# A two-layer graph network in one kernel: order of work at the ends of layer 0's chunks, PSUM of the stage between the layers, and the place of the last split

## The chip, the cores and the metric

The kernel runs on one NeuronCore of a Trainium2 chip. The core has a matrix engine (TensorE, PE in the profile, with its weight loads shown apart as PEld), a vector engine (VectorE, DVE), an activation engine (ScalarE, ACT), a general engine (GpSimd, POOL) and the sync engine (SyncE, SP), which here issues nearly all DMAs. Work passes through SBUF (128 partitions) and through PSUM[...], into which TensorE writes. The metric is the device time of one execution in microseconds; lower is better.

## What is computed

Layer 0 is attention over all 4096 rows with a dense additive bias, layer 1 a graph attention with eight heads of 64. Cut to what matters:

```python
# layer 0
h = relu(layernorm(x))                      # x: 4096 x 512, adj: 4096 x 4096
q, k, v = h @ Wq.T + bq, h @ Wk.T + bk, h @ Wv.T + bv
x = x + softmax(q @ k.T / sqrt(512) + adj + adj, axis=-1) @ v
# layer 1, heads n of 64
h = relu(layernorm(x))
nX = heads(h @ W)
nX = a_ln * (nX - mean(nX)) / (std(nX, ddof=1) + 1e-6) + b_ln
at1, at2 = nX @ a1, nX @ a2                 # one number per row and head
kg = leaky_relu(at1[:, None] + at2[None, :], 0.2) * adj
y = softmax(where(adj != 0, kg, -32768), axis=-1) @ nX + nX
x = x + elu(y)
```

## The kernel before

**Tiling.** Rows are handled in 8 chunks (`NI`) of 512 (`GC`), columns in 32 blocks (`NB`) of 128 (`P`). `seq` keeps the instructions it wraps in program order on their engine, so the order of the calls below is the order on each engine and on each DMA queue. Tiles come from pools; a tag with `bufs=n` has n buffers that rotate. A pool opened in the room of a closed one waits for the closed one's last users.

**Projections** (up to line 546): the values, the products of queries and keys, and their sums for a Strassen-like scheme are made and written to DRAM. Their pool's last stores are the `q_d` stores of line 477.

**Layer 0** (lines 547 to 789) goes over all chunks, and in each over 16 pairs of column blocks. For a pair `s`, `stage(s, n, w)`, n = 0 to 3, forms the logits: seven products of half size go to the two halves of one PSUM bank, `xz` (`w["z"]` and `w["x"]`), and `add_part` (line 593, DVE) adds them to the transposed adjacency tile `aT`; `exponent0` (line 597, ACT) makes probabilities; `pair_sums` (lines 609 to 621, POOL) makes sums of them and the running row totals. `weighted(s, ...)` (line 636, PE) adds the pair's products into seven PSUM accumulators `M1` to `M7`, which stay for a whole chunk. The loop interleaves: while pair s is weighted, pair s + 2 passes its four stages, and the tiles of s + 4 and s + 5 are transposed (`swap`, line 324) and prepared for layer 1 (`for_layer_1`, lines 575 to 579, DVE, with two stores each). Where the first pair is concerned, its stages run alone, before the loop.

**Chunk end.** At a chunk's last pair, `chunk_end` puts six parts into the list `ends`, each one or two operations that combine M1 to M7 into rows of the result (line 691: the first on ACT, the others on DVE). `end()` runs the next one. In the last pair they run after stage 0, after stage 1, before the weighted products of M6 and M3, and after stage 3; the last two in the next pair. `total_of_rows` (lines 709 to 719) sums the row totals over partitions with four tiny products against `ones`, into a tile of M6's tag, and takes reciprocals; it runs in the next chunk's first pair, after the sixth part, and for the last chunk after the loop. `divide` (lines 679 to 688) scales the rows and adds x by a DMA.

**Stage between the layers** (lines 1221 to 1258): for each block r of 128 rows: `turn` (transposes, then a relu on ACT), `project` (16 matmuls into `ys[r]`, two banks, tag "l" with two buffers), `variance` (square on ACT, then lines 1110 and 1111 on DVE, then a power of -1/2 on POOL, line 1112), `standardize` (lines 1119 to 1134 on DVE, then line 1139 on POOL, the tile `own`). The order in the loop is turn(r + 1), project(r), standardize(r - 1), variance(r). Tasks hang at blocks (`at_block`): `split(ic)` (lines 1147 to 1169, fourteen DVE steps on a chunk's at1 and at2), `sides(ic, b)` (line 1181 on PE, line 1186 on ACT, three stores each, lines 1188 and 1192), `fours` (lines 1196 to 1200), `load_targets` (line 1204, four loads of `at2m`), stores of features and own rows (lines 1210 and 160). Those of the last chunk that come after block 32 are moved with `at_step` to the first steps of layer 1.

**Layer 1** (from line 1267) has 512 steps: chunk, group of four heads, block. Step n: `sums` (PE, lines 874 and 904, into PSUM tiles l, r0, r1), the tasks of `left`, `left_sums(n + 1)` (line 884), `right_leaky` (line 922, DVE), `right_weigh` (line 928, POOL), `left_relu` (line 890, ACT), `values` of step n - 4 (line 947, PE), tasks marked "mid", `left_weigh` (line 931, DVE), `exponent` (line 935, ACT), tasks marked "end". Every four steps SP issues the loads of the next four (`load_adj`, lines 815 to 830: z2, nb, nx, g; two buffers each), and in the first 32 steps also the features `nX` (line 1058).

## Time and profile before

Median of 3 runs: 3674.54 us (3672.04 to 3674.67). The profiled execution took 3674.76 us; its span, which all times below are counted in, is 3672.7 us.

| what | value |
|---|---|
| PE busy | 3551.3 us, 97% of the span |
| DVE busy | 2548.8 us, 69% |
| POOL busy | 2263.0 us, 62% |
| ACT busy | 1745.0 us, 48% |
| mean rate of all DMAs | 217 GB/s |
| costliest on PE | L947, `values`, 1009.9 us |
| costliest on POOL | L928, `right_weigh`, 1223.1 us |
| stage between the layers | about 1861 to 2036 us |

A line such as "L691 DVE TENSOR_TENSOR x<-x,M" names the kernel's line, the engine, the operation and the tiles it writes and reads. "[0.57 <-DVE x L691]" behind an instruction says how long its engine stood idle before it and which instruction let it go. Such a name is inferred from the times of the events. Busy shares are means over stretches that have different limits, so the reading below goes stretch by stretch. Matmul ends are modelled: an idle time between two runs of matmuls is counted from the modelled end of the first, while a steady row of them starts at shorter distances than its durations.

### The profile page before, as it was taken

Reading aid. Unit: us, or ns where it says so; the run is one execution under the profiler, and the core shown is the slowest. Engines: PE = TensorE matmul, PEld = TensorE weight load, DVE = VectorE, ACT = ScalarE, POOL = GpSimd, SP = SyncE. Lnnn points to the kernel's source line nnn. Section 1 sums busy time; section 2 is a strip of 40 time slices with the busy share of each in tenths; the row PEclk is TensorE's granted clock in tenths of the full one; section 3 lists DMA queues with packets and bytes.
Section 4 is the critical chain, followed back from the end, with each engine's and each line's share of the span. In section 5 each row is a group of like instructions: output and inputs, shape, how many; then the busy total and the mean of one; then the engine's idle time right before and its main releaser. Section 6 shows DMA issues by size and latency. Waiting matters only on the chain. (4 is left out here: it accounts for less than half of the span.)

```text
span 3672.7 us, 58831 instructions
## 1 busy us (share of the span) xinstructions
PE 3551.3 (97%) x21482; PEld 2084.0 (57%) x21482; DVE 2548.8 (69%) x4195; ACT 1745.0 (48%) x1541; POOL 2263.0 (62%) x1770
## 2 busy tenths in 40 slices
PE   8998999999999999999988799999999999999998
PEld 3447888888888888888866223322222223322332
DVE  5435565666666665656556678888888888888887
ACT  1000111111111111111123589998999999989997
POOL 4653445454545454444445568887888888877886
PEclk9999999999999999999999899999999999999999
DMA  6567788888888888888758987887787787778775
GB/s 213 180 207 203 230 242 239 238 242 244 237 234 250 237 237 243 241 249 232 217 143 207 214 220 211 211 212 201 211 209 212 203 213 204 209 198 214 211 210 151
DMA packets 667530, 796.85 MB, mean 217 GB/s; under 512 B 86816, under 2 KB 489696, under 8 KB 658016
## 3 DMA queue, kind: packets, MB, share of 16 engines
q1 hardware_dynamic: 655136, 759.64, 73.6%
q0 software_dynamic: 10704, 31.98, 4.8%
q8 instruction: 171, 2.80, 0.3%
q10 hardware_dynamic: 1392, 1.38, 0.1%
q14 instruction: 127, 1.04, 0.1%
HBM read 602.28 MB, written 182.71 MB: 214 GB/s over the span
## 5 line engine op out<-in xcount | busy, mean ns | idle before, releaser
L928 POOL TENSOR_TENSOR t<-t,g 128x1024 f32<-128x1024 f32 x512 | 1223.1, 2398 | 318.0 <-DVE t L922 242.4
L947 PE MATMUL acc<-t,nX 128*64 128x512 f32 x4096 | 1009.9, 609 | 0.0
L935 ACT ACTIVATE t<-t 128x2048 f32<-128x2048 f32 (+1 forms) x527 | 976.6, 1854 | 0.2 <-POOL t L928 0.2
L922 DVE SCALAR_TENSOR_TENSOR t<-u,at2m,r 128x512 f32<-128x512 f32 x1024 | 718.6, 743 | 209.3 <-issue 145.3
L597 ACT ACTIVATE aT<-aT 128x512 f32<-128x512 f32 x256 | 161.2, 630 | 1415.7 <-DVE aT L593 1415.7
L593 DVE TENSOR_TENSOR aT<-aT,XZ 128x256 f32<-128x256 f32 x896 | 352.9, 417 | 596.8 <-PE XZ L585 592.4
L931 DVE TENSOR_TENSOR t<-l,g 128x1024 f32<-128x1024 f32 x512 | 622.5, 1216 | 20.7 <-DMA g<-gT_d 16.7
L890 ACT ACTIVATE l<-l 128x1024 f32<-128x1024 f32 x512 | 516.5, 1009 | 149.4 <-PE l L884 101.5
L947 PEld LDWEIGHTS acc<-t,nX 128*64 128x64 f32 x4096 | 248.0, 136 | 458.3 <-issue 450.7
L585 PE MATMUL XZ<-qt,hS 128*128 128x256 f32 x2048 | 488.2, 382 | 9.6 <-DVE aT L593 9.6
L585 PEld LDWEIGHTS XZ<-qt,hS 128*128 128x128 f32 x2048 | 390.6, 191 | 64.1 <-DVE aT L593 11.1
L609 POOL TENSOR_TENSOR S<-aT 128x256 f32<-128x256 f32 x128 | 93.0, 726 | 525.8 <-ACT aT L597 525.8
L585 PE MATMUL XZ<-qt,hT 128*128 128x256 f32 x1536 | 374.3, 380 | 4.6 <-DVE aT L593 3.8
L621 POOL TENSOR_TENSOR total<-total,aT 128x256 f32<-128x256 f32 x360 | 326.5, 919 | 9.4
L585 PEld LDWEIGHTS XZ<-qt,hT 128*128 128x128 f32 x1536 | 291.3, 190 | 47.9 <-DVE aT L593 7.2
L874 PEld LDWEIGHTS <-z 6*128 6x128 bf16 x2048 | 52.4, 91 | 433.1 <-DVE t L922 350.2
L610 POOL TENSOR_TENSOR aT<-aT 128x256 f32<-128x256 f32 x128 | 93.0, 726 | 287.3 <-ACT aT L597 287.3
L636 PE MATMUL M<-v,aT 128*128 128x256 f32 x1024 | 263.0, 379 | 0.0
L636 PE MATMUL M<-tv,aT 128*128 128x256 f32 x1024 | 262.7, 379 | 0.0
L636 PE MATMUL M<-v,S 128*128 128x256 f32 x1024 | 242.0, 379 | 0.0
L577 DVE SCALAR_TENSOR_TENSOR gs<-ng,aT 128x512 f32<-128x512 bf16 x256 | 225.7, 882 | 8.8
L884 PE MATMUL l<-z_left,z 64*64 64x512 bf16 x2048 | 203.0, 383 | 26.8 <-DVE t L931 17.1
(178 smaller groups left out, 4372.0 us busy)
## 6 DMA issues: line engine op xcount, KB each, us to landing
g<-gT_d SPq DMA_DIRECT2D x128, 1024.0 KB
ag<-in_adj_dram SPq DMA_DIRECT2D x256, 256.0 KB
hS<-s_d SPq DMA_DIRECT2D x64, 1024.0 KB
gT_d<-gs SPq DMA_DIRECT2D x256, 256.0 KB
nb<-nT_d SPq DMA_DIRECT2D x128, 512.0 KB
nx<-nT_d SPq DMA_DIRECT2D x256, 256.0 KB
hT<-h_d SPq DMA_DIRECT2D x64, 768.0 KB
tv<-vt_d SPq DMA_DIRECT2D x128, 384.0 KB
```

What stands on the lines that cost most here:

```text
L577: seq(nc.vector.scalar_tensor_tensor(gs, ng, G_MASKED / NEG_BIG, aT, ALU.mult, ALU.add))
L585: seq(nc.tensor.matmul(out, a, b, start=start and k == 0, stop=k == 1, skip_group_check=not start,))
L593: seq(nc.vector.tensor_add(p, p, part))
L621: seq(nc.gpsimd.tensor_add(t, t, a))
L636: seq(nc.tensor.matmul(sums[ic][i][:, u, :], a[:, ts(u, P)], b, start=jt == 0 and u == 0, stop=jt == NB - 2, skip_group_check=u == 1,))
L884: seq(nc.tensor.matmul(lefts[n][ts(c, HD), r, :], loads[n // JB][2][ts(r, HD), jt % JB * P + c * HD :][:, :HD], groups[ic, hg]["z1_left"][ ...
L890: seq(nc.scalar.activation(lefts[n], lefts[n], AF.Relu, scale=4.0))
L922: seq(nc.vector.scalar_tensor_tensor(t[:, 2 + e, :], u4[:, e, :], at2m[:, jt, h : h + 1], right[e], ALU.max, ALU.add))
L928: seq(nc.gpsimd.tensor_mul(t[:, 2:4, :], t[:, 2:4, :], both_heads(n)))
L931: seq(nc.vector.tensor_mul(logits[n][:, 0:2, :], lefts.pop(n), both_heads(n)))
L935: seq(nc.scalar.activation(t, t, AF.Exp))
L947: seq(nc.tensor.matmul(grp["acc"][hf][ts(e, HD), :], nX[jt // SB][:, jt % SB, hg * HG + 2 * hf + e, :], t[:, hf + 2 * e, :], start=jt == 0 ...
```

## The change

- `ones` is made once at the start, outside the pool of layer 0.
- The first pair of all gets its `z` in a bank of its own (M3's tag), so its products alternate between two banks.
- In a chunk's last pair the third part of the chunk end runs after stage 3, directly before the fourth. `total_of_rows` runs after stage 2 instead of before it, and M3's weighted products come ahead of M6's. For the last chunk `total_of_rows` uses the `xz` bank and runs before the remaining parts.
- The stage between the layers gets a PSUM pool of its own: one bank for the transposes, three pairs of banks for the projections, one bank for `sides` and `fours`. It is closed before layer 1's pool is opened.
- In `variance` the division by 63 moves into the square's scale; the lower bound 1e-30 is taken on POOL, ahead of the power, and no longer on DVE.
- The last chunk's `split` runs at the end of step 1 of layer 1; its store of at2 at step 2, `fours` and the first `sides` at step 3, the other three `sides` in the middle of steps 5, 7 and 9 in the bank of r1, `load_targets` at step 5.

```diff
@@ -126,6 +126,8 @@
     HB = HD + 1
     back = const.tile([P, 2, HB], F32, name="back")
 
+    ones = const.tile([P, 1], F32, name="ones")
+    nc.vector.memset(ones, 1.0)
     low0 = const.tile([P, SB], F32, name="low0")
     high0 = const.tile([P, SB], F32, name="high0")
     nc.vector.memset(low0, -LOWEST)
@@ -547,8 +549,6 @@
         with tc.tile_pool(name="attn", bufs=2) as work, tc.tile_pool(
             name="attn_ps", bufs=2, space=PSUM
         ) as psum:
-            ones = work.tile([P, 1], F32, name="ones", tag="ones", bufs=1)
-            nc.vector.memset(ones, 1.0)
             later = {}
             turned, probs, sums, rows_of, totals = {}, {}, {}, {}, {}
 
@@ -646,13 +646,14 @@
 
 
                 if n == 0:
-                    w["z"], w["x"] = xz[:, 0], xz[:, 1]
+                    w["x"] = xz[:, 1]
+                    w["z"] = w["alone"] if "alone" in w else xz[:, 0]
                     product(w["z"], s, "A12", "B21", True)
                     product(w["x"], s, "A11", "B11", True)
                     add_part(s, 0, w["z"])
                     add_part(s, 0, w["x"])
                 elif n == 1:
-                    product(w["z"], s, "S1", "T1", False)
+                    product(w["z"], s, "S1", "T1", "alone" in w)
                     product(w["x"], s, "S2", "T2", False)
                     add_part(s + 1, 1, w["z"])
                     add_part(s, 1, w["x"])
@@ -707,7 +708,10 @@
                     rests.append(divide)
 
             def total_of_rows(ic):
-                pt4 = psum.tile([P, 2, H], F32, name="pt4", tag="M6", bufs=1)[:, 0, 0:SB]
+                if ic + 1 < NI:
+                    pt4 = psum.tile([P, 2, H], F32, name="pt4", tag="M6", bufs=1)[:, 0, 0:SB]
+                else:
+                    pt4 = xz[:, 0, 0:SB]
                 total = totals.pop(ic)
                 for b in range(SB):
                     seq(nc.tensor.matmul(
@@ -723,7 +727,7 @@
                 swap(s)
                 for_layer_1(s)
             load_sums(0)
-            w = {}
+            w = {"alone": psum.tile([P, 2, H], F32, name="z0", tag="M3", bufs=1)[:, 0]}
             for n in range(4):
                 stage(0, n, w)
             pair_sums(0)
@@ -763,15 +767,13 @@
                     stage(s + 2, 1, w)
                 end()
                 weighted(s, (4, 1), (5, 0), (5, 1))
-                if jt == 0 and ic:
-                    total_of_rows(ic - 1)
                 if more:
                     stage(s + 2, 2, w)
                 if jt == NB - 4 and ic + 1 < NI:
                     load_chunk(ic + 1, nc.sync, range(4, 7))
-                if last_pair:
-                    end()
-                weighted(s, (6, 0), (6, 1), (3, 0), (3, 1))
+                if jt == 0 and ic:
+                    total_of_rows(ic - 1)
+                weighted(s, (3, 0), (3, 1), (6, 0), (6, 1))
                 if ahead:
                     swap(s + 5)
                     for_layer_1(s + 5)
@@ -779,13 +781,14 @@
                     stage(s + 2, 3, w)
                 if last_pair:
                     end()
+                    end()
                 if more:
                     pair_sums(s + 2)
                 for f in later.pop(s, []):
                     f()
+            total_of_rows(NI - 1)
             while ends:
                 end()
-            total_of_rows(NI - 1)
             rests[0]()
 
 
@@ -796,7 +799,8 @@
         name="ga_in", bufs=2
     ) as inputs, tc.tile_pool(name="gat", bufs=1) as gat, tc.tile_pool(
         name="ga", bufs=2
-    ) as work, tc.tile_pool(name="ga_ps", bufs=2, space=PSUM) as psum:
+    ) as work, ExitStack() as banks:
+        psum = banks.enter_context(tc.tile_pool(name="stage_ps", bufs=2, space=PSUM))
         JB = 4
         STEPS = [(ic, hg, jt) for ic in range(NI) for hg in range(NH // HG) for jt in range(NB)]
         n_steps = len(STEPS)
@@ -1084,14 +1088,13 @@
             seq(nc.sync.dma_start(out=xns[ic], in_=by_blocks(xn_d, ic)))
 
         def turn(r):
-            tag = f"r{r % 2}"
-            m = psum.tile([P, GC], F32, name=tag, tag=tag, bufs=1)
+            m = psum.tile([P, GC], F32, name="turned", tag="turned", bufs=1)
             for k in range(KC):
                 seq(nc.tensor.transpose(m[:, ts(k, P)], xns[r // SB][:, r % SB, ts(k, P)], ident))
             seq(nc.scalar.activation(h1s[:, r % 2], m, AF.Relu))
 
         def project(r):
-            ys[r] = psum.tile([P, 2, GC], F32, name="l", tag="l", bufs=2)
+            ys[r] = psum.tile([P, 2, GC], F32, name="y", tag="y", bufs=3)
             for g in range(2):
                 for k in range(KC):
                     seq(nc.tensor.matmul(
@@ -1102,14 +1105,15 @@
         def variance(r):
             ic, b = r // SB, r % SB
             seq(nc.scalar.activation(
-                sqs[:, r % 2].rearrange("p (g h) e -> p g (h e)", g=2), ys[r][:, :, 0 : D // 2], AF.Square
+                sqs[:, r % 2].rearrange("p (g h) e -> p g (h e)", g=2), ys[r][:, :, 0 : D // 2],
+                AF.Square, scale=1.0 / math.sqrt(HD - 1.0),
             ))
             v = prep.tile([P, NH], F32, name="var", tag="var", bufs=2)
             root = prep.tile([P, NH], F32, name="pw", tag="pw", bufs=2)
             deviating[r] = v, root
             seq(nc.vector.tensor_reduce(v, sqs[:, r % 2], AX.X, ALU.add))
-            seq(nc.vector.tensor_scalar(v, v, 1.0 / (HD - 1.0), 1e-30, ALU.mult, ALU.max))
-            seq(nc.gpsimd.tensor_tensor(root, v, mhalf[:, 0:NH], ALU.pow))
+            seq(nc.gpsimd.tensor_scalar_max(root, v, 1e-30))
+            seq(nc.gpsimd.tensor_tensor(root, root, mhalf[:, 0:NH], ALU.pow))
 
         def standardize(r):
             ic, b = r // SB, r % SB
@@ -1150,9 +1154,13 @@
             at2s = prep.tile([P, SB, NH], F32, name="at2s", tag="at2s", bufs=2)
             seq(nc.vector.tensor_scalar_mul(at2s, at[:, :, 1, :], -4.0))
             rows = slice(ic * SB, (ic + 1) * SB)
-            at_block(SB * ic + 5, lambda: seq(nc.sync.dma_start(
-                out=at2_d[rows].rearrange("q p h -> p q h"), in_=at2s
-            )))
+            def store_targets():
+                seq(nc.sync.dma_start(out=at2_d[rows].rearrange("q p h -> p q h"), in_=at2s))
+
+            if ic + 1 < NI:
+                at_block(SB * ic + 5, store_targets)
+            else:
+                at_step(2, store_targets)
             at1s = prep.tile([P, SB, NH], F32, name="at1s", tag="at1s", bufs=2)
             seq(nc.vector.tensor_scalar_mul(at1s, at[:, :, 0, :], 4.0))
             at2c = prep.tile([P, SB, NH], F32, name="at2c", tag="at2c", bufs=1)
@@ -1173,9 +1181,13 @@
                         left = rest
             at1ss[ic] = at1s
 
-        def sides(ic, b):
-            tag = f"acc{b % 2}"
-            m = psum.tile([P, GC], F32, name=tag, tag=tag, bufs=1)
+        def one_bank(tag):
+            return banks_now[0].tile([P, GC], F32, name="m", tag=tag, bufs=1)
+
+        banks_now = [psum]
+
+        def sides(ic, b, tag="side"):
+            m = one_bank(tag)
             r = ic * SB + b
             for kind in range(4):
                 seq(nc.tensor.matmul(
@@ -1191,8 +1203,8 @@
                 ))
             seq(nc.sync.dma_start(out=z1_d[:, :, ts(r, P)], in_=zc[:, 2:4, :]))
 
-        def fours(ic):
-            m = psum.tile([P, GC], F32, name="acc1", tag="acc1", bufs=1)[: SB * NH, 0:P]
+        def fours(ic, tag="side"):
+            m = one_bank(tag)[: SB * NH, 0:P]
             seq(nc.tensor.transpose(m, at1ss[ic].rearrange("p b h -> p (b h)"), ident))
             u4c = prep.tile([SB * NH, P], F32, name="u4c", tag="u4c", bufs=2)
             seq(nc.scalar.copy(u4c, m))
@@ -1220,11 +1232,12 @@
 
         for ic in range(NI):
             r = SB * ic + 4
-            at_block(r, split, ic)
+            if ic + 1 < NI:
+                at_block(r, split, ic)
             at_block(r + 1, store_features, ic)
             for n in range(4):
                 at_block(r + 2 + n // 2, lambda ic=ic, n=n: store_rows(own_d, ic, owns[ic], n))
-            at_block(r + 3, load_targets, ic)
+            at_block(r + 3 if ic + 1 < NI else r + 5, load_targets, ic)
             if ic + 1 < NI:
                 for b in range(SB):
                     at_block(r + 1 + b, sides, ic, b)
@@ -1253,9 +1266,14 @@
         for r in after:
             for f in at_blocks.pop(r):
                 at_step(r - NB, f)
-        at_step(1, fours, NI - 1)
-        for b in range(SB):
-            at_step(2 + b // 2, sides, NI - 1, b)
+        banks.close()
+        psum = banks.enter_context(tc.tile_pool(name="ga_ps", bufs=2, space=PSUM))
+        banks_now[0] = psum
+        later.setdefault((1, "end"), []).append(lambda: split(NI - 1))
+        at_step(3, fours, NI - 1, "acc0")
+        at_step(3, sides, NI - 1, 0, "acc1")
+        for b in range(1, SB):
+            later.setdefault((3 + 2 * b, "mid"), []).append(lambda b=b: sides(NI - 1, b, "r1"))
         left_sums(0)
         left_relu(0)
 
```

## The prediction

> **What bounds the kernel now.** I read the table by stretches first, to give every stretch its limit. Columns: stretch and length, busy us (and count) of PE, its weight loads, DVE, ACT and POOL, then the TensorE clock, DMA share, GB/s.
>
> ```profile
> 300.00:1850.00 1550.00, 1541.76 (x7155) 1354.02 (x7154) 937.70 (x1782) 200.63 (x318) 721.18 (x941) 1.00 0.83 236
> 1861.00:2036.00 175.00, 147.97 (x771) 118.12 (x771) 113.28 (x397) 53.61 (x104) 96.38 (x73) 0.98 0.72 184
> 2036.00:2055.00 19.00, 12.64 (x85) 3.71 (x81) 13.41 (x27) 9.91 (x11) 10.25 (x5) 0.50 0.99 262
> 2055.00:2067.00 12.00, 8.69 (x44) 1.98 (x44) 4.46 (x6) 5.64 (x4) 2.70 (x2) 0.69 0.65 140
> 2067.00:2136.00 69.00, 60.95 (x456) 17.15 (x452) 47.79 (x62) 52.61 (x38) 44.64 (x19) 0.95 1.08 227
> 2155.00:3655.00 1500.00, 1480.63 (x12074) 445.38 (x12071) 1262.81 (x1583) 1381.69 (x1011) 1215.59 (x558) 1.00 0.79 208
> ```
>
> Layer 0's pairs and layer 1 after 2155 us are TensorE's, without a gap to win but the seams. The stage between them (1861 to 2036) fills no engine, so a chain bounds it. The first steps of layer 1 are the DMA's (share about 1), with a hole of 12 x 0.35 = 4.2 us at 2055 to 2067. Then I read the timelines of the engines at each seam. Start, duration, instruction; in brackets the idle time before it and what ended it. A chunk end of layer 0, PE then DVE:
>
> ```profile
> 1078.23 1.99 PE L585 MATMUL XZ<-qt,hT 128*128 128x256 f32 x8 [0.42 <-DVE aT L593]
> 1085.54 1.02 PE L713 MATMUL pt<-ones,total 128*128 128x1 f32 x8 [0.57 <-DVE x L691]
> ...
> 1074.63 1.40 DVE L691 TENSOR_TENSOR x<-x,M 128x512 f32<-128x512 f32 x2
> 1077.76 0.41 DVE L593 TENSOR_TENSOR aT<-aT,XZ 128x256 f32<-128x256 f32 x1
> 1084.72 1.27 DVE L691 TENSOR_TENSOR x<-x,M 128x512 f32<-128x512 f32 x2
> ```
>
> The third part of the chunk end (1074.63) pushes the last XZ addition to 1078.17, and the row totals, written into M6's bank, wait until the sixth part has read M6. The first pair:
>
> ```profile
> 278.17 0.06 DVE L551 MEMSET ones<- 128x1 f32 x1 [5.26 <-DMA q_d<-qs]
> 282.72 3.78 PE L585 MATMUL XZ<-qt,hS 128*128 128x256 f32 x8 [7.76 <-DVE aT L593]
> 287.35 3.69 PE L585 MATMUL XZ<-qt,hS 128*128 128x256 f32 x8 [0.84 <-DVE aT L593]
> 291.89 1.13 PE L585 MATMUL XZ<-qt,hT 128*128 128x256 f32 x4 [0.84 <-DVE aT L593]
> ```
>
> One period of the stage, POOL and DVE:
>
> ```profile
> 1879.88 0.17 DVE L1119 TENSOR_TENSOR nq<-pw,var 128x8 f32<-128x8 f32 x1 [1.81 <-POOL pw L1112]
> 1881.76 1.27 POOL L1139 TENSOR_TENSOR own<-feat,aln_sb 128x512 f32<-128x512 f32 x1 [1.92 <-DVE at L1134]
> 1882.39 0.67 DVE L1111 TENSOR_SCALAR var<-var 128x8 f32<-128x8 f32 x1
> 1883.21 1.64 POOL L1112 TENSOR_TENSOR pw<-var,mhalf 128x8 f32<-128x8 f32 x1 [0.17 <-DVE var L1111]
> 1884.88 0.17 DVE L1119 TENSOR_TENSOR nq<-pw,var 128x8 f32<-128x8 f32 x1 [1.81 <-POOL pw L1112]
> ```
>
> The start of layer 1, DVE and the SP queue:
>
> ```profile
> 2035.62 1.31 DVE L1147 TENSOR_TENSOR at<-at,at_b 128x64 f32<-128x64 f32 x1
> 2039.50 1.40 DVE L922 SCALAR_TENSOR_TENSOR t<-u,at2m,r 128x512 f32<-128x512 f32 x2
> 2058.12 2.19 SPq L1204 DMA_DIRECT2D at2m<-at_d  x4
> 2063.77 0.55 SPq L815 DMA_DIRECT2D z<-z_d  x1
> ```
>
> **What the Trainium skill says.** "SBUF — State Buffer", section "Who interferes with whom": a DVE instruction with two SBUF inputs, or one in a two-port mode, is blocked by a GpSimd instruction that started first. The trace agrees: L1111 takes 0.17 us alone (1901.27) and 0.67 beside own, ending with it at 1883.05. "PSUM — Partial Sum Buffer", section "PSUM bank collisions raise a hardware error": guard by bank, not by address. The program does: the product at 282.72 starts only after both additions out of XZ (281.80 to 282.67). "TensorE: Matmul & The Clock Gate", section "What's actually happening": about 3.4 us of idleness halves the clock; after the 4.68 us gap before 2040.96 the same matmuls take 0.64 instead of 0.38. "DMA: Bandwidth & Descriptors", section "Rules for kernel authors": under 64 KB one pays mostly overhead; beside the 32 and 64 KB z stores the rate falls to 140 GB/s.
>
> **The change part by part**, against the profiled execution (span 3672.7, its own time 3674.76, which is 0.22 above the median shown, 3674.54).
>
> *First pair.* Moving `ones` saves its 0.06 us only: its wait is the new SBUF pool's for the old one (the q_d stores), and the transpose L324 behind it inherits it. With z in M3's bank, a product no longer waits for the other's addition. Z may start at 282.30 instead of 282.72, and four products of 1.72 (4 passes at the 0.43 pitch there) run through to 289.2. The last product waits for x's addition (0.2 drain + 0.41 + 0.05): 289.85 against 291.89. That is 2.0; the loads behind it move along, bar some. I take -1.8 (0 to -2.2).
>
> *Chunk ends.* Pairs start every 12.09 us (565.23, 577.32, 589.41), a chunk takes 693.99 to 889.77 = 195.78, and 16 x 12.09 + 0.89 for the totals is 194.33: 1.45 is lost at each of seven ends. The first stall is 0.58 (1078.23 against 1065.56 + 12.09), the second 0.73 (1083.51 + 1.30 = 1084.81 against 1085.54). Both go. The third part runs after stage 3, beside the fourth: 2.8 us of DVE from 1076.97 to 1079.7, while stage 0's product ends at 1079.5. M2, M5 and M4 are still free before PE comes to them. The totals come after stage 2 at about 1086, when M6 has long been read (sixth part's first half, 1084.9); their reciprocals (0.5 us) lie under the 0.86 of M3's products, put ahead of M6's. Next in line is stage 2, with no margin against stage 1's additions: I leave 0.1 there. 7 x 1.3 = -9.1 (-6 to -9.8).
>
> *End of layer 0.* The totals go to XZ before the last additions. TensorE no longer waits 2.98 us for them, but the division (L681, 1857.83) and the next PSUM pool still wait for the eight additions, which end 0.2 earlier than the reciprocals did: -0.2.
>
> *The stage.* The bounding chain is, in one period of 5.00: five small DVE steps 1.11, feat 0.69, own 1.27 (+0.08), then pow 1.64 with 0.2 of gaps. Three y pairs, one transposed bank and the scale inside the square are off it: PE idles 27 us of 175 here, relu frees its bank (1876.86) long before the next transposes (1880.54), and the single side bank makes PE wait for one 0.58 us copy per chunk. The DVE step that goes (0.67) ended with own, so it hid. The clamp comes to POOL between own and pow: the nearest row, L279's 128x4 step, takes 0.24 and 0.09 to the next, in place of the 0.17 gap; its size could double it. I take +0.1 in 24 plain blocks = +2.4 (0 to +8). Seven blocks with a split (5.9) gain 0.1 each, since L1147 stays blocked until own ends: -0.7. The block at 1897 to 1903 waited 0.9 through a cold project at 1894.40 that had no free pair: -0.9. Sum +0.8.
>
> *Start of layer 1.* The last split (2035.62 to 2039.5) leaves the front, but the new PSUM pool waits for the old one as at 1858.12, so PE begins at 2035.7 where before it began at 2031.2, and step 0 gains about 1 us only. The split comes back behind step 1, partly under right_weigh (2.35). What counts is the SP queue. At 2048.32 a store waits for the eighth DMA before it (g), so about eight are in flight, and 23 DMAs stand between the loads for q = 1 and q = 2; 10 will. Own's stores follow the features' directly, and the loads of q = 2 leave about 2058 to 2060 instead of 2063.77 to 2069. That closes most of the 4.2 us hole. The 13 moved (at2m at step 5; z at 5, 7 and 9) make a new one between the loads of q = 2 and q = 3 of 2 to 3 us. ACT's three 0.58 us copies and r1's wait hide while the DMA limits. I take -2.0 (-8 if nothing reopens and the waits of steps 4 to 6 go too; +3 if the new hole is larger).
>
> Sum: -1.8 - 9.1 - 0.2 + 0.8 - 2.0 = -12.3; 3674.54 - 12.3 = 3662.2, forecast 3662.
>
> **Rivals.** (1) The start of layer 1 opens fully: 6 us more, 3656. For it: steps 4 to 6 stand 6.2, 3.7 and 2.4 us on DVE. Against it: the DMA share is 1.08 from 2067 on. (2) The stage's period falls by the removed 0.67 in 31 blocks: 21 us more, 3641. For it: L1111 stands in the row of that chain. Against it: own ends at the same moment. (3) The chunk ends give half, because DVE's two parts in a row delay stage 0's or stage 2's additions, and the first pair's gain is eaten by its loads: 3662 + 4.5 + 1.8 = 3668. (4) Slower: SP is in order, so a z store of steps 5, 7 and 9 that waits for its step holds the next big loads; if each of the six remaining groups slips by one step (2.97 us, as in the later steps), that is +18, the gain of 2 goes too, and 3682 results. It decides from 12 us on. Against it: those loads wait for the same steps' buffers anyway.
>
> **How the numbers follow.** Forecast 0.58 (3657 to 3668), rivals 0.16, 0.06, 0.11, 0.09. About 0.2% (7.3 us) is what a measurement of this kernel can tell from no change, so faster means below 3667.2: 0.54 of the forecast's 0.58, 0.16, 0.06 and 0.01 of rival 3 make 0.77; the rest of the first and third, 0.14, is same; slower 0.09. The range, 3654 to 3672, leaves out rival 2, rival 4 and the ends of the parts.
>
> **What would show it.** No XZ wait and no totals wait at a chunk end, chunks of 194.5; last product of the first pair 2 us earlier; the small DVE step L1119 every 5.1 us; q = 2's loads before 2061, counted from the stage's end. A period below 4.9 us, or first steps longer than now, would make it wrong.

## The result and the profile after

The changed kernel takes 3664.66 us (median of 14 runs, 3655.05 to 3680.39) against 3674.61 us before (14 runs, 3657.54 to 3685.51): ratio 0.9977, with a 95% interval of 0.9961 to 0.9994. Timed once more beside the kernel before (e11 below) it took 3663.17 us, ratio 0.9951 (0.9935 to 0.9968). It is some 10 us faster in the first comparison and 16 in the second; 3662 was forecast. Its profiled execution took 3669.51 us, its span is 3667.7 (before: 3672.7). Single executions of the changed kernel lie from 10 us below its median to 16 above it, so the parts below are read from stretches of the profiles and not from totals. The "mark" below is the last block's first small DVE step (2033.70 before, 2027.69 after); from it the start of layer 1 is counted. Lines have moved: L1119 of before is L1123 now, L922 is L926, L691 is L692, L713 is L717.

First the table by stretches of the changed kernel (columns as in the prediction; the last three are the granted TensorE clock, the busy share of the DMA engines and GB/s). The last three rows are slices of 10 us counted from each kernel's step 0, the first of them from the kernel before:

```profile
1860.00:2028.00 168.00, 134.85 (x709) 111.71 (x707) 93.16 (x351) 51.58 (x98) 101.33 (x101) 0.96 0.69 179
2036.00:2055.00 19.00, 12.26 (x69) 2.85 (x61) 12.51 (x27) 10.31 (x9) 7.79 (x4) 0.52 0.91 250
2055.00:2067.00 12.00, 11.68 (x100) 3.42 (x102) 9.54 (x14) 9.64 (x9) 9.46 (x4) 1.00 0.91 202
2067.00:2106.00 39.00, 35.76 (x283) 10.21 (x280) 29.84 (x39) 33.65 (x25) 27.54 (x12) 1.00 1.00 232
2106.00:2157.00 51.00, 43.01 (x302) 12.18 (x300) 31.39 (x41) 34.61 (x26) 29.37 (x13) 0.90 0.99 215
...
2059.50:2069.50 10.00, 7.25 (x48) 1.82 (x48) 4.51 (x7) 4.18 (x4) 4.71 (x2) 0.83 0.70 160
2062.84:2072.84 10.00, 10.00 (x88) 2.81 (x80) 7.75 (x11) 9.37 (x9) 7.79 (x4) 1.00 0.73 161
2122.84:2132.84 10.00, 9.43 (x76) 2.73 (x74) 8.01 (x11) 8.80 (x7) 7.13 (x3) 1.00 0.58 120
```

The stage still fills no engine. The start of layer 1 ran 6 us earlier this time, so 2055 to 2067 is not the place of the old hole in the transfers, which is 20 to 30 us behind the mark (a share of 0.68 before, 0.76 after, see below); TensorE is busy at 2055 to 2067 for 11.68 of 12 us. But it is idle for 8 us of 51 later, at 2106 to 2157. The share of 0.99 there is a mean: it is 1.07 and more for most of the time, and 0.58 in the 10 us from 2122.84.

The first pair and a chunk end, timeline of PE:

```profile
281.06 2.08 PE L585 MATMUL z<-qt,hS 128*128 128x256 f32 x4 [7.31 <-DVE aT L593]
282.93 1.91 PE L585 MATMUL XZ<-qt,hS 128*128 128x256 f32 x4
284.64 1.69 PE L585 MATMUL z<-qt,hS 128*128 128x256 f32 x4
286.17 1.03 PE L585 MATMUL XZ<-qt,hS 128*128 128x256 f32 x4
287.71 1.13 PE L585 MATMUL XZ<-qt,hT 128*128 128x256 f32 x4 [0.51 <-DVE aT L593]
...
1074.05 1.89 PE L585 MATMUL XZ<-qt,hS 128*128 128x256 f32 x8
1077.37 1.99 PE L585 MATMUL XZ<-qt,hS 128*128 128x256 f32 x8
1079.20 0.95 PE L717 MATMUL pt<-ones,total 128*128 128x1 f32 x8
```

After the wait for the transpositions four products of the first pair run through without a bracket, and the last comes 10.74 us after DVE's first transposition at 276.97 (before: 291.89 - 278.17 = 13.72). At the chunk end neither the XZ product nor the totals carry a bracket. The totals stand at 884.52, 1079.20, 1273.88: a period of 194.68 against 195.78. (Five of the six periods of this profile are 194.68; the one that ends at 884.52 is 195.50.) What is left of the stall is at 1077.37, where stage 2 begins 3.32 after the stage ahead of it; in a pair without a chunk end that is 3.02.

One period of the stage, DVE and POOL:

```profile
1957.72 0.17 DVE L1123 TENSOR_TENSOR nq<-pw,var 128x8 f32<-128x8 f32 x1 [2.79 <-POOL pw L1116]
1962.98 0.17 DVE L1123 TENSOR_TENSOR nq<-pw,var 128x8 f32<-128x8 f32 x1 [2.79 <-POOL pw L1116]
...
1959.60 1.27 POOL L1143 TENSOR_TENSOR own<-feat,aln_sb 128x512 f32<-128x512 f32 x1 [1.92 <-DVE at L1138]
1960.95 0.24 POOL L1115 TENSOR_SCALAR pw<-var 128x8 f32<-128x8 f32 x1
1961.28 1.67 POOL L1116 TENSOR_TENSOR pw<-pw,mhalf 128x8 f32<-128x8 f32 x1
```

The period is 5.26 to 5.27 us, not 5.00. Own ends at 1960.87, the power begins at 1961.28: 0.41 for the clamp and the gaps on both its sides, where before 0.18 lay between own and power. The power takes 1.67 instead of 1.64.

SP's queue at the start of layer 1:

```profile
2048.50 0.55 SPq L819 DMA_DIRECT2D z<-z_d  x1
2055.29 5.94 SPq L1216 DMA_DIRECT2D at2m<-at_d  x4
2062.23 1.55 SPq L1200 DMA_DIRECT2D z_d<-zc  x2
2064.49 0.56 SPq L1204 DMA_DIRECT2D z_d<-zc  x1
2067.35 0.55 SPq L819 DMA_DIRECT2D z<-z_d  x1
```

The loads for q = 2 leave 20.8 us after the mark instead of 30.1 (2063.77 - 2033.70). Behind them stand the loads of the targets, whose issue takes 5.94 us, and z stores; the loads for q = 3 leave only 18.9 us after those for q = 2. The old hole is smaller and a new one is there: 35 to 40 us behind the mark the share is 0.61, before it was 1.05.

### The profile page after: what moved, and what is told of

Its sections match the earlier page's. It is cut to its first block, busy times and chain, and to the rows that moved or that the text cites. A ratio compares the mean times of both kernels' runs of the same rounds, so it can differ in the third digit from the quotient of the medians.

```text
span 3667.7 us, 58811 instructions
## 1 busy us (share of the span) xinstructions
PE 3546.0 (97%) x21482; PEld 2085.7 (57%) x21482; DVE 2536.0 (69%) x4163; ACT 1746.5 (48%) x1541; POOL 2269.8 (62%) x1802
## 5 line engine op out<-in xcount | busy, mean ns | idle before, releaser
L926 DVE SCALAR_TENSOR_TENSOR t<-u,at2m,r 128x512 f32<-128x512 f32 x1024 | 719.2, 744 | 205.6 <-issue 150.0
```

The costliest lines, as they stand in the source:

```text
L926: seq(nc.vector.scalar_tensor_tensor(t[:, 2 + e, :], u4[:, e, :], at2m[:, jt, h : h + 1], right[e], ALU.max, ALU.add))
```

## The experiments

The stretches compared in the tables below lie between these points: the first and the last block's first small DVE step (L1123), the first t of layer 1 (step 0), and the t of step 56, where all kernels run at TensorE's pace. Not every part was tried apart: the place of `ones`, the order of M3 and M6, the last totals in the `xz` bank and the scale inside the square were not.

### Chunk ends: one of the two moves at a time

e5, the third part early again:

```diff
                 if jt == 0 and ic:
                     total_of_rows(ic - 1)
+                if last_pair:
+                    end()
                 weighted(s, (3, 0), (3, 1), (6, 0), (6, 1))
...
                 if last_pair:
                     end()
-                    end()
```

> The changed kernel with the third part of a chunk's end back ahead of stage 3's additions; the totals and the order of the products stay as changed. Theory: the third part (1.40 us of DVE) delayed the last XZ addition and cost TensorE 0.58 at the next stage 0; the chunk's period goes from 194.68 to about 195.2 or 195.3, and a wait of about 0.4 for DVE stands before the XZ product that follows. Rival: with the totals out of the way DVE has room, and the period stays at 194.7.

e6, the totals early again:

```diff
+                if jt == 0 and ic:
+                    total_of_rows(ic - 1)
                 if more:
                     stage(s + 2, 2, w)
...
-                if jt == 0 and ic:
-                    total_of_rows(ic - 1)
                 weighted(s, (3, 0), (3, 1), (6, 0), (6, 1))
```

> The changed kernel with the row totals back ahead of stage 2; the third part stays late. Theory: the totals are written into M6 and wait for the sixth part's first half, a stall of about 0.6 to 0.7 per chunk; the period goes from 194.68 to about 195.3. Rival: part of that stall was handed on by the first one (0.58) and is gone with it, so the period stays below 194.9.

One profiled execution each. Timeline of PE of e5, then of e6, at a chunk end:

```profile
875.39 1.99 PE L585 MATMUL XZ<-qt,hT 128*128 128x256 f32 x8 [0.42 <-DVE aT L593]
```

```profile
883.67 1.02 PE L717 MATMUL pt<-ones,total 128*128 128x1 f32 x8 [0.82 <-DVE x L692]
```

In e5 the totals stand at 883.85 and 1078.97, a period of 195.12: +0.44. In e6 they stand at 883.67 and 1079.01: 195.34, +0.66. Both waits come back where they were, and 0.44 + 0.66 = 1.10 is the whole of what the change saved. The two losses add up, so neither move needs the other. e5's period grew by less than the expected 0.5 to 0.6, because stage 2's own stall of 0.30 all but goes when the third part no longer runs ahead of it (882.02 follows 878.95 by 3.07): the move trades part of one stall for the other. The single times of these two runs, 3669.51 and 3683.71, say nothing of it: e6's stretch from step 56 to the end took 12.7 us longer than the changed kernel's (1448.6 against 1435.9), in code that is the same.

### First pair without a bank of its own

e7 puts z and x back into the two halves of one bank (`xz`, 128 x 512 f32):

```diff
-            w = {"alone": psum.tile([P, 2, H], F32, name="z0", tag="M3", bufs=1)[:, 0]}
+            w = {}
```

> The changed kernel without the bank of its own for the first pair's z (z and x in the two halves of XZ again). Theory: the first pair's last product starts 13.7 us after DVE takes up the first transposition, as in the kernel before, instead of 10.7; three us, two for the additions that each product waits for and about one because the products with gaps run longer at the halved clock. Rival: the clock has nothing to do with it, and the difference is the 2.0 us that the prediction worked out (12.7).

Timeline of PE of e7 (one execution, 3669.14 us):

```profile
281.49 3.78 PE L585 MATMUL XZ<-qt,hS 128*128 128x256 f32 x8 [7.75 <-DVE aT L593]
286.12 1.99 PE L585 MATMUL XZ<-qt,hS 128*128 128x256 f32 x8 [0.84 <-DVE aT L593]
288.96 1.13 PE L585 MATMUL XZ<-qt,hT 128*128 128x256 f32 x4 [0.84 <-DVE aT L593]
```

The waits are those of the kernel before, but the second pair of products takes 1.99 us and not 3.69: the last product stands 12.02 us after the first transposition (276.94), below the 13.7 of the one theory and the 12.7 of the other. Neither had it. With z alone, twelve executions (after, e1 to e6, e8 to e12) give 10.23 to 10.94. So the bank is worth 1.1 to 1.8 us against this one execution without it, and 1.7 of the 3.0 between the two first profiles is the moment at which the clock came back. The granted clock shows it, in windows of before and then of after:

```profile
286.00:292.00 6.00, 4.31 (x11) 2.64 (x10) 1.50 (x4) 0.41 (x1) 0.00 (x0) 0.60 0.00 0
286.00:292.00 6.00, 5.49 (x26) 4.52 (x25) 3.90 (x7) 1.26 (x2) 2.55 (x3) 1.00 0.07 23
```

The clock's records put its return at 290.82 in before, 285.97 in after and 285.61 in e7, which is 12.6, 9.0 and 8.7 us behind the first transposition. "TensorE: Matmul & The Clock Gate", section "What's actually happening", says that the window over which activity is judged runs freely, so that the number of slow matmuls differs from run to run; the 3.69 and 1.99 us for the same eight matmuls, with the same waits ahead of them, agree.

### The clamp

e3 takes the lower bound on DVE again, in place:

```diff
-            seq(nc.gpsimd.tensor_scalar_max(root, v, 1e-30))
-            seq(nc.gpsimd.tensor_tensor(root, root, mhalf[:, 0:NH], ALU.pow))
+            seq(nc.vector.tensor_scalar_max(v, v, 1e-30))
+            seq(nc.gpsimd.tensor_tensor(root, v, mhalf[:, 0:NH], ALU.pow))
```

> The changed kernel with the clamp at 1e-30 on DVE, in place, as a single maximum; the scale stays in the square. Theory: the clamp on GpSimd (0.24 us and a second gap of 0.09, and a power of 1.67 in place of 1.64) is the whole of the longer period; on DVE it ends with own and the period is 5.00 again, the stage 24 x 0.27 = 6.5 us shorter (162.5 us from the first to the last block instead of 169.1). Rival: the longer period comes from the third pair or the PSUM layout; then it stays at 5.27.

Median 3662.06 us of 19, ratio to before 0.9972 (0.9961 to 0.9983). Timeline of POOL and DVE of e3:

```profile
1949.24 1.27 POOL L1143 TENSOR_TENSOR own<-feat,aln_sb 128x512 f32<-128x512 f32 x1 [1.92 <-DVE at L1138]
1950.68 1.64 POOL L1116 TENSOR_TENSOR pw<-var,mhalf 128x8 f32<-128x8 f32 x1 [0.17 <-DVE var L1115]
...
1950.05 0.49 DVE L1115 TENSOR_SCALAR var<-var 128x8 f32<-128x8 f32 x1
1952.35 0.17 DVE L1123 TENSOR_TENSOR nq<-pw,var 128x8 f32<-128x8 f32 x1 [1.81 <-POOL pw L1116]
```

The clamp on DVE ends with own (1950.54 against 1950.51) and costs nothing; the period is 4.99 to 5.00 again, with the third pair and the new layout in place. From the first small step to the last block's: 163.06 us, against 169.14 with the clamp on GpSimd and 163.81 before. The clamp is the whole of the longer stage, and the third pair and the new layout have no part in it. The times are too rough to show these 6 us: e4 below, which was timed in the same series and has the clamp on GpSimd, took 3664.83.

### The place of the last split

e4 puts the last split, its targets and its sides where they stood before:

```diff
...
-            if ic + 1 < NI:
-                at_block(r, split, ic)
+            at_block(r, split, ic)
...
-        later.setdefault((1, "end"), []).append(lambda: split(NI - 1))
-        at_step(3, fours, NI - 1, "acc0")
-        at_step(3, sides, NI - 1, 0, "acc1")
-        for b in range(1, SB):
-            later.setdefault((3 + 2 * b, "mid"), []).append(lambda b=b: sides(NI - 1, b, "r1"))
+        at_step(1, fours, NI - 1, "acc1")
+        for b in range(SB):
+            at_step(2 + b // 2, sides, NI - 1, b, f"acc{b % 2}")
```

> The changed kernel with the last chunk's split, the store and load of its targets and its z stores where they stood before (split in the stage's last block, sides at steps 2 and 3); the rest as changed. Theory of the prediction: the start of layer 1 then stands 2 us later, with the hole in the transfers between the loads for q = 1 and q = 2, and step 36 comes about 142 us after the last block's first small DVE step. Rival: the start of layer 1 is limited by transfers until about 130 us after the stage, so that what the moved split gains in the first 60 us is given back; step 36 then stands within 1.5 us of where it is with the split moved (141.7 us after the last block's first small step).

e11 is the changed kernel once more.

> The changed kernel itself, for a second profile of the start of layer 1 and more times beside the kernel before. Theory: the time from the last block's first small DVE step to step 56 differs between executions of the same code by about 2 us (204.1 in the changed kernel's profile, 201.9 with the clamp on DVE), so the moved split's effect, 203.6 before, cannot be read from one profile; this run gives 202 to 205. Rival: it gives 204.1 within 0.3, and the moved split costs half a microsecond in place of the 2.0 that the prediction had it gain.

| run | split | mark to step 0 | step 0 to step 56 | both |
|---|---|---|---|---|
| before | in stage | 5.80 | 197.84 | 203.64 |
| e4 | in stage | 5.89 | 196.63 | 202.52 |
| after | moved | 5.15 | 198.95 | 204.10 |
| e11 | moved | 5.15 | 198.29 | 203.44 |
| e3 | moved | 5.16 | 196.71 | 201.87 |
| e5 | moved | 5.15 | 194.56 | 199.72 |
| e6 | moved | 5.16 | 196.12 | 201.28 |
| e7 | moved | 5.15 | 199.60 | 204.76 |

Step 0 gains 0.65 to 0.73, as the split is gone from in front of it; at step 56 the six profiles with the split moved stand at 199.7 to 204.8, the two with it in the stage at 203.6 and 202.5. Step 36 comes 140.2 us after the mark in e4 and 141.7 in the changed kernel. The scatter of some 5 us is larger than the whole term, so e11's rival (204.1 within 0.3) fails and e4's theory (2 us later) is not borne out: moved or not, the start is the same within what can be seen.

The holes did move. In all six profiles with the split moved the loads for q = 2 leave 20.8 us after the mark, in e4 26.5. From 20 to 30 us behind the mark the share is 0.62 in e4; from 35 to 40 us it is 1.07 in e4 and 0.26 to 0.68 in the six. e4's median, 3664.83 (ratio 0.9979, 0.9971 to 0.9988), is the changed kernel's.

### What sets the stage's period

e1 issues a block's variance ahead of the previous block's standardization, so that GpSimd makes the power before own; e2 is e1 with two projection pairs in place of three (`bufs=2`).

```diff
+            if 0 <= r < NB:
+                variance(r)
             if r >= 1:
                 standardize(r - 1)
-            if 0 <= r < NB:
-                variance(r)
```

> The changed kernel with one thing moved: block r's variance (its sum, clamp and power) is issued ahead of block r-1's standardization, so that GpSimd makes the power before the previous block's own. Theory: in the changed kernel the stage's period of 5.27 us (GpSimd own 1.27, clamp 0.24, power 1.67, then five small DVE steps and feat) is a chain through GpSimd, and TensorE with about 4.05 us of work a block only waits. Then the period falls: to about 4.3 us if TensorE takes over as the bound (stage 30 us shorter), to about 4.75 us if the five small DVE steps are held up by the power that now runs beside them (16 us shorter); the run stands 16 to 30 us below the changed kernel, at 3635 to 3649. Rival: the period is not set by that order (TensorE, its banks or the loads set it); it stays at 5.2 to 5.3 and the time at 3665.

> The same with two projection pairs (y, bufs=2) in place of three. Theory: with the power first, the projection of a block is read about 2.7 us after it is made (sum 0.7, five steps 1.1, feat and at 0.9), so the third pair is what lets TensorE go on; with two pairs each projection waits for it and the period is about 6.5 us or at least 1 us above that of the run with three. Rival: the third pair does nothing here either, as the prediction said of the change, and both periods agree within 0.1 us.

e1: median 3664.15 us of 11, ratio 0.9975 (0.9964 to 0.9986). e2: 3721.52 us of 4, ratio 1.0139 (1.0119 to 1.0158). Timeline of DVE and PE of e1, then of PE of e2:

```profile
1861.96 0.16 DVE L1123 TENSOR_TENSOR nq<-pw,var 128x8 f32<-128x8 f32 x1
1865.96 0.16 DVE L1123 TENSOR_TENSOR nq<-pw,var 128x8 f32<-128x8 f32 x1
...
1964.60 0.40 PE L1193 MATMUL m<-ident_b,parts 128*128 128x128 bf16 x4 [3.02 <-DVE parts L1175]
```

```profile
1949.07 3.83 PE L1100 MATMUL y<-w_sb,h1s 128*128 128x264 f32 x16 [2.55 <-DVE at L1138]
```

The first blocks of e1 take 4.00 us, TensorE's own work, and no small step waits for POOL: the order own, clamp, power was what set 5.27. But from the first split on TensorE, which is in order, waits 3.02 us for the split's last piece, and a chunk takes 21.3 or 23.0 us in turn (21.6 in the changed kernel). The 1.7 us between the two are the clock: after every second of these waits it fell to half, and the projection behind took 5.41 us (at 1942.26) in place of 3.73 (at 1965.27). Only 5.4 us of the stage are gained (168.9 instead of 174.3 up to step 0; 16 to 30 were expected), and the time does not show them. In e2 the period is 6.98 to 7.05 in most blocks and 8.5 to 8.7 in the first and a few others: 30 projections wait 2.3 us on average until the pair of two blocks back has been read. So the third pair carries e1's order. In the changed kernel's order it does nothing for a plain block: the period is 5.00 with two pairs (before) and with three (e3).

e8 is e1 with the readers of a split moved away from it:

```diff
-                for b in range(SB):
-                    at_block(r + 1 + b, sides, ic, b)
-                at_block(r + 3, fours, ic)
+                at_block(r + 2, fours, ic)
+                for b in range(SB):
+                    at_block(min(r + 2 + b, r + 4), sides, ic, b)
```

> The run with the power first (e1), with the products that read a split moved away from it: fours at block 4ic+6 instead of 4ic+7, the four sides at blocks 4ic+6, +7, +8 and +8 instead of +5 to +8. Theory: in e1 the plain blocks took 4.00 to 4.23 us, TensorE's own work, but TensorE is in order and waited 3 us a chunk for the split (m after parts) and again behind it, which gave the gain back; with a block between, a chunk's four blocks take about 18.7 us instead of 22.2, the stage is 20 to 25 us shorter than e1's, and the time about 3640 to 3648. Rival: the transfers of the stage (their share was 0.72 at 175 us) or DVE's 14.9 us a chunk become the bound, or the start of layer 1 gives it back because its transfers then have less time: the stage is shorter but the time stays above 3655.

Median 3653.26 us of 7, ratio 0.9952 (0.9933 to 0.9972). The stage up to step 0 is 149.72 us, 19.2 shorter than e1's (20 to 25 were expected, and a time of 3640 to 3648). TensorE's waits in one chunk of e8, timeline of PE:

```profile
1956.73 0.38 PE L1193 MATMUL m<-ident_b,parts 128*128 128x128 bf16 x4 [0.71 <-ACT u4c L1210]
...
1967.22 0.38 PE L1193 MATMUL m<-ident_b,parts 128*128 128x128 bf16 x4 [1.65 <-ACT zc L1198]
```

Both are two users of the one side bank directly behind each other; in the second ACT's copy also waited 0.60 us for a store out of zc. e9 was to part them, with six buffers for zc (so also e10 and e12):

```diff
+            for f in ahead_of.pop(r, []):
+                f()
             if r + 1 < NB:
                 turn(r + 1)
...
-                at_block(r + 2, fours, ic)
-                for b in range(SB):
-                    at_block(min(r + 2 + b, r + 4), sides, ic, b)
+                ahead_of.setdefault(r + 2, []).append(lambda ic=ic: fours(ic))
+                for b in range(3):
+                    at_block(r + 2 + b, sides, ic, b)
+                ahead_of.setdefault(r + 4, []).append(lambda ic=ic: sides(ic, 3))
```

> The run e8 with no two products into the one side bank directly behind each other: fours and the fourth side are issued ahead of the next block's transposition, a projection away from the other side; zc gets six buffers in place of four. Theory: in e8 a chunk took 18.99 us, of which 0.71 and 1.65 were waits of TensorE for the copy out of the side bank; without them it takes 17.0 to 17.5, the stage is 10 to 14 us shorter again. At the start of layer 1 about a quarter of e8's shorter stage was given back (6 of 24 us); if that share holds, the time is 3642 to 3648. Rival: the transfers needed by the first steps of layer 1 now set the time alone; then all of the further gain is given back and the time stays at 3653.

Timeline of PE of e9:

```profile
1962.08 0.39 PE L1193 MATMUL m<-ident_b,parts 128*128 128x128 bf16 x4
1963.41 0.38 PE L1193 MATMUL m<-ident_b,parts 128*128 128x128 bf16 x4 [0.94 <-ACT zc L1198]
```

It missed: what is put ahead of block r's transposition stands directly behind the side that ended block r - 1. In the stage TensorE waits 7.2 us for the side bank (13.4 in e8), but 4.3 for the split, which fours now meets too early. A chunk takes 18.98 us as in e8, the stage 149.23. The time is 3650.38 us (6 runs), ratio 0.9925 (0.9904 to 0.9945). e10 also issues the last chunk's z stores from another queue:

```diff
+            queue = nc.sync if ic + 1 < NI else nc.gpsimd
...
-                seq(nc.sync.dma_start(
+                seq(queue.dma_start(
```

> The run e9 with the last chunk's twelve z stores issued from GpSimd's queue in place of SP's. Theory of the prediction: z stores standing ahead of the loads in SP's order open holes in the transfers of the first 50 us of layer 1; without them the loads of q = 1 to 3 leave earlier and the stretch from step 0 to step 56 is 2 to 5 us shorter than e9's. Rival: the stretch is limited by the bytes to be moved (share above 1 in most of it) and by GpSimd, which issues the stores between its own operations; the stretch stays within 2 us or grows.

Median 3648.34 us of 5, ratio 0.9907 (0.9889 to 0.9926); step 0 to step 56 takes 203.29 us, against 199.93 in e9. The loads for q = 3 and q = 4 do leave earlier, 45.4 and 54.0 us after the mark instead of 50.4 and 63.0, as the theory had it, but the stretch did not get shorter. With one profile of each and a scatter of 5 us, the theory's 2 to 5 us are not seen, and not excluded; the two times cannot be told apart. e12 is e8 with fours (block 4ic+6) and the fourth side (block 4ic+8) between the halves of that block's projection:

```diff
         def project(r):
             ys[r] = psum.tile([P, 2, GC], F32, name="y", tag="y", bufs=3)
             for g in range(2):
+                if g:
+                    for f in between.pop(r, []):
+                        f()
...
```

> The run e8 with fours and each chunk's fourth side issued between the two halves of a projection (e9 had put them ahead of the next transposition, where the side of the block before still stood directly ahead of them: its chunks took 18.98 us and kept a wait of 0.94 for the side bank); zc with six buffers as in e9. Theory: now some 2 us of matmuls stand between two users of the side bank, the waits go, a chunk takes 17.0 to 17.5 us and the stage is 8 to 13 us shorter than e9's 149.2 (first block's small step to step 0); the time is 3640 to 3647. Rival: the transfers (share 0.81 to 0.85 in e8's stage) or DVE's work become the bound and the stage stays above 145 us, or the start of layer 1 gives all of it back and the time stays at 3650.

Median 3650.41 us of 6, ratio 0.9929 (0.9907 to 0.9950). Timeline of PE of e12:

```profile
1951.84 0.39 PE L1198 MATMUL m<-ident_b,parts 128*128 128x128 bf16 x4
1955.14 1.04 PE L1093 MATMUL turned<-ident,xns 128*128 128x128 f32 x4 [2.91 <-DMA xns<-xn_d]
1955.97 5.04 PE L1105 MATMUL y<-w_sb,h1s 128*128 128x264 f32 x16
```

The waits for the side bank have nearly gone (1.6 us in the whole stage; 7.2 in e9), and most chunks take 17.9 us (17.0 to 17.5 were expected), in which TensorE is idle for 0.5. Two waits come in their place: in two chunks the loads of the layer's input come too late, 5.1 us together, and five projections wait 4.9 us together for a pair of banks. Behind the gap of 2.91 us shown here the clock fell to half, and the projection takes 5.04 us instead of 3.73. The stage is 1.0 shorter than e9's instead of 8 to 13, so the rival (the stage stays above 145) was right, by the transfers in part.

| run | stage, first small step to step 0 | step 0 to step 56 | sum |
|---|---|---|---|
| after | 174.29 | 198.95 | 373.24 |
| e1 | 168.89 | 201.50 | 370.39 |
| e8 | 149.72 | 205.58 | 355.30 |
| e9 | 149.23 | 199.93 | 349.16 |
| e10 | 150.08 | 203.29 | 353.37 |
| e12 | 148.18 | 209.67 | 357.85 |

Table by stretches of e9: the stage, and 77 us of layer 1 from 50 us after step 0:

```profile
1860.71:2009.94 149.23, 130.99 (x724) 107.92 (x726) 102.88 (x362) 52.18 (x98) 101.39 (x102) 0.98 0.76 197
2060.00:2137.00 77.00, 68.15 (x498) 19.21 (x497) 52.60 (x67) 58.18 (x42) 47.51 (x21) 0.93 1.05 244
```

The rates over the stretches, multiplied by their lengths, give about 75 MB between the two outer marks in the changed kernel, in e8, in e9 and in e12 alike (for e9: 149.23 x 197 + 50.06 x 221 + 77 x 244 + 72.87 x 213 GB/s). Whatever the stage saves, these bytes have to move in less time, and in the first 130 us of layer 1 the transfers are nearly full (a share above 1 in most slices of 10 us). That this is the reason for what follows is an inference; no run changed the bytes. From step 0 to step 56 the four profiles of e8, e9, e10 and e12 take 204.6 us on average, the six profiles with the split moved, in the table further up, 197.4: some 7 of the 24 to 26 us off the stage are given back there. The times of the four, 3648 to 3653, come from different series, in which the kernel before took 3671 to 3680 (medians). In the one series that had the changed kernel beside them (e11), e9 is 12.8 us faster and e10 14.8. e8 is 17.5 us faster than the kernel before, about as much as e11 (16.5), so a gain of e8 over the changed kernel is not shown. Where the rest of the 24 to 26 us goes was not followed.

## Why the prediction was right, and where it was not

The measured time lies in the range and 2.7 us from the forecast. That it came so close is in part luck, as the terms show. By the prediction's own terms, from the two profiles:

| term | predicted | measured |
|---|---|---|
| first pair | -1.8 (0 to -2.2) | -2.98 |
| seven chunk ends | -9.1 (-6 to -9.8) | -7.3 from the first pair's last product to the last XZ addition (7 x 1.10 would be -7.7; one chunk took 0.8 longer) |
| end of layer 0, last XZ addition to first small step | -0.2 | 22.32 to 22.41: +0.1, a clamp in it |
| stage, first to last block | +0.8 | 163.81 to 169.14: +5.3 |
| start of layer 1, to step 56 | -2.0 (-8 to +3) | 203.64 to 204.10: +0.5, within the scatter |
| sum | -12.3 | -4.4 |

*First pair.* Right in mechanism: the wait for the q_d stores was inherited, z ran ahead and the products ran through. e7 puts the bank at 1.1 to 1.8, beside 1.8 forecast; the excess over it is the clock, which the prediction's sum had at half speed throughout.

*Chunk ends.* Right: both waits gone, and next in line was stage 2, as said. Its stall was sized at 0.1 and is 0.30: of the 1.45 lost at an end 1.10 came back instead of 1.3. 194.5 was forecast, 194.68 came. Each of the two moves is shown by its own run (e5, e6).

*The stage.* The mis-sized term. The chain was named rightly (own, clamp, power, small steps), so the removed DVE step brought nothing and rival 2 fell. But the clamp was put at +0.1 in 24 blocks, and the small steps at every 5.1 us; they came every 5.26 to 5.27. The prediction's own row gave 0.24 + 0.09 - 0.17 = 0.16, and it forgot the gap between own and clamp (0.08): 0.41 - 0.18 = 0.23, and 0.03 more for the power, make the measured 0.26 to 0.27, or about 6.4 us in 24 blocks instead of 2.4 (still inside its 0 to +8). Six of the seven blocks with a split gained 0.1 each (5.91 to 5.81 in five of them), as worked out; the second went from 6.30 to 6.57. The block that waited for a cold projection takes a plain block's 5.26 instead of 5.90, as worked out (5.00 in e3), though the third pair was not tried apart in this order. With the clamp away (e3) the stage is 0.75 us shorter than before, about this one block.

*Start of layer 1.* The order of events was right: step 0 earlier by 0.7 (1 was forecast), the loads for q = 2 at 20.8 us, the old hole smaller, a new one between q = 2 and q = 3. That this is worth 2 us was not shown: the steps ran 5 us ahead of the kernel before at step 8 (38.6 us after the mark instead of 43.6) and had lost it by step 32. Little of that lead is the moved split's, for e4, with the split in the stage, is at 39.8 at step 8. The prediction named first steps longer than now as a sign against it: the first four took 20.8 us, before 19.4; the next four made up for it (12.6 against 18.4). What was lost by step 32 was lost mainly in two stalls of TensorE, around 2110 and 2140, with shares of 1.09 and 1.08; ahead of the second, at 2121.8 to 2127.2, SP stood still for 5.3 us in front of a load of u, and the share fell. Profiles of before and of e4 have such a hole there too.

The rivals: 1 and 2 are excluded by the start (no 6 us) and the period (no 0.67). Rival 3's loss at the chunk ends is not there. Rival 4's z stores do stand in the queue, but cost less than the scatter.

Two readings of the prediction don't hold. The gap of 4.68 us before 2040.96 did not halve the clock: the clock's record has it at half from 2035.03 on, and the matmuls at 2035.64, ahead of that gap, take 0.64 already. Nor do the gaps of this case keep to the 3.4 us of idleness that the prediction quotes: the clock fell around one of 2.56 us in before (record at 1895.09) and one of 2.91 in e12 (1955.20), but not after each of e1's gaps of 3.0. And the 140 GB/s beside the z stores do not show overhead of small transfers: 140 at a share of 0.65 is 215 for full engines, against 265 in the stretch ahead (262 at 0.99) and 210 in the one behind (227 at 1.08), where no such stores are. The engines had less to do.

The terms sum to -4.4. With 1.2 us by which the first pair came earlier and 0.6 by which the code behind step 56 took longer, both in unchanged code, that is the -5.0 of the two spans, but not the medians (-10 in the first comparison, -16 beside e11). The stage came 4.5 us worse than forecast, the start of layer 1 2.5 and the chunk ends 1.8, the first pair 1.2 better; that the median met 3662 within 2.7 us all the same is owed to some 5 us that no term accounts for. The stretch from step 56 to the end, in unchanged code, took 1435.4 us before, 1435.9 and 1436.2 in the two profiles of the changed kernel, 1432.0 in e1, 1442.6 in e3. Where those 5 us are stays open: one profile of before is too few to say.

## What to carry to other kernels

When a small step is moved to another engine, count the gap on each side of it and ask whether it falls between two links of the chain: 0.24 us on GpSimd cost 0.27 a period here, where 0.67 us of DVE beside own had cost nothing. If a chain through a shared engine sets a period, look first for the order of its links (power before own) and then for what the in-order engine meets next; here every step of that search uncovered the next bound: the split, the side bank, then the loads and the pairs of banks. A stretch that is nearly full of transfers can take back a part of what a stretch ahead of it saves (some 7 of 25 us here), so the later one has to be looked at before the earlier is shortened. And a lead over a single profile of the kernel before proves little: here the same code differed by 5 us over 200, and one more profile, with the part in question put back, undid the reading.

## What the runs showed of the hardware that was not expected

The same eight matmuls of the first pair took 3.69 us in one execution and 1.99 in another, with the same waits ahead of them; the moment of the clock's return alone is worth 1.7 us there. The clock was at half for 13.65 us around the first pair in before, for 10.24 in e10 and for 6.83 in the other twelve profiles: all multiples of 3.41. In the stage of e1, gaps of 3.0 us cost the clock in every second chunk only, so the same gap is sometimes free and sometimes costs 1.7 us more. And the power of 128x8 on GpSimd took 1.67 us where it followed the clamp and wrote over its input, against 1.64 from another tile.
